# Edges of an attention stage: the last tile's softmax sums on the tensor engine, and the second image's normalisation moved forward

## The chip, the cores and the metric

The kernel runs on one core of a Trainium2 chip. A core has five engines with queues of their own: TensorE (PE, with weight loads shown as PEld), VectorE (DVE), ScalarE (ACT), GpSimd (POOL) and SyncE (SP), which here issues nearly all DMAs. The engines run side by side and wait for each other through semaphores. The metric is the device time of one execution in microseconds (us), lower being better; a profile is one execution recorded instruction by instruction.

## The reference

Two layers work on x of shape (2, 256, 64, 64), that is two images of 256 channels and 4096 tokens. Layer 0 is a Mamba block with an MLP behind a group norm. Layer 1 is attention with 8 heads of 32 channels behind another group norm. Only layer 1 is touched here:

```python
def _L1_conv_ref(x, qkv_w, qkv_b, num_heads):
    ...
    qkv = jnp.einsum('bchw,oc->bohw', x, qkv_w) + qkv_b[None, :, None, None]
    qkv = qkv.reshape(b, 3, num_heads, head_dim, n)
    q, k, v = (qkv[:, 0], qkv[:, 1], qkv[:, 2])
    scale = 1.0 / math.sqrt(head_dim)
    attn_logits = jnp.einsum('bhci,bhcj->bhij', q, k) * scale
    attn_weights = jax.nn.softmax(attn_logits, axis=-1)
    out = jnp.einsum('bhij,bhcj->bhci', attn_weights, v)
    return out.reshape(b, c, h, w)
...
x = x + _L1_conv_ref(_gn(x), L1_conv_qkv_w, L1_conv_qkv_b, 8)
```

## The kernel before

`conv_preact_kernel` runs `mamba_stage` for both images (to about 1993 us of the profile), then `attention`, then `out_of_range`, a check that decides whether a slower general version must run (it isn't run on this data). Inside `attention` the order of instructions on every engine is the order in which the code writes them (`tc.manual_schedule`), so the code is read as a schedule.

Attention takes an image as KG x NT = 16 query tiles: two groups of four heads, each with eight tiles of 512 queries. A tile walks over NC = 32 chunks of 128 keys, and a chunk has two halves of two heads each. For each half `logits` (L1162) makes scores on TensorE into one of three PSUM buffers `s`; `exponentials` (L1175) makes their exponentials on ScalarE; `values` (L1199) multiplies by v into `po`, 32 output rows for each head. The sums of the exponentials over the keys, the softmax's denominators, are gathered by `add_up`. Heads 0 and 1 are written into a buffer `chunk` that holds four terms side by side. After every third key chunk VectorE sums the four terms in one instruction (`sum_chunk`, L1184) into the first place of the next `chunk` buffer. There are two such buffers, so ScalarE can write into a buffer again only once the sum that read it is done. Heads 2 and 3 are added one by one: on GpSimd into `acc_p` (L1230, L1232), and for some chunks (SHARED) head 2 on VectorE into `acc_2` in PSUM (L1229).

When a tile is done, `finish` works through it in steps that are laid between the next tile's chunks by `side`: `Slots.run` is called once for each key chunk, and a step's `yield n` asks for the next one n turns later. The steps copy `po` out of PSUM (L1240), put the partial sums together (L1242, L1243), sum over the 128 key rows with a matrix of ones on TensorE (L1250), copy that out (L1253), take reciprocals in four pieces (L1257), multiply (L1260, on GpSimd except for the very last tile), add bias and the residual (L1263), store (L1264), and keep the largest sum and reciprocal for the range check (L1266, L1267).

For image 0, q, k and v were prepared by the Mamba stage. For image 1 they are made in `prepare`, between the two images: `load_x` (L1032) brings x, `normalise` (L1036) applies the group norm, `project` (L1046) makes q or k, `project_values` (L1067) makes v. The first two x tiles share one `q` buffer. The norm's two scales come from `group_norm_scales`: VectorE aggregates statistics (L39), TensorE averages over the channels of a group (L43), VectorE forms the spread (L45 to L51), TensorE averages again (L55), ScalarE takes a logarithm and an exponential (L58, L59). This generator is also run by `side`, from the first chunks of image 0. The loads and the first normalisation for image 1 are put into image 0's last tile by lines in `run`:

```python
                        if b == 0 and s == S - 8:
                            load_x(0)
                            load_x(1)
                        if b == 0 and s == S - 4:
                            normalise(0)
```

Here s counts key chunks over all tiles and S is their number, so S - 8 is chunk 24 of the last tile.

Of the kernel before, what the change touches and what calls it, by code (L numbers as in the profile page):

```python
# [11 lines left out]
F32 = mybir.dt.float32  # L12
F32R = mybir.dt.float32r
AF = mybir.ActivationFunctionType
ALU = mybir.AluOpType
AX = mybir.AxisListType
# [3 lines left out]
P = 128  # L20
T = 512
GROUP = 8
HEADS = 8
D = 32
QUAD = 4
KG = HEADS * D // P
# [3 lines left out]
def group_norm_scales(nc, small, psum_tile, stats, gmat, eps_t, out):  # L30

    KC = stats.shape[1]
    mv = [small.tile([P, 2], F32, name=f"gn_mv{k}") for k in range(KC)]
    e = [small.tile([P, 2], F32, name=f"gn_e{k}") for k in range(KC)]
    out += [small.tile([P, 2], F32, name=f"gn_sc{k}") for k in range(KC)]
    for k in range(KC):
        nc.vector.bn_aggr(mv[k], stats[:, k, :, :].rearrange("p a s -> p (a s)"))  # L39
    yield 2  # L40
    ps = psum_tile()
    for k in range(KC):
        nc.tensor.matmul(ps[:, k : k + 1], lhsT=gmat, rhs=mv[k][:, 0:1], start=True, stop=True)  # L43
    for k in range(KC):
        nc.vector.tensor_copy(out[k][:, 0:1], ps[:, k : k + 1])  # L45


    for k in range(KC):
        nc.vector.tensor_sub(e[k][:, 0:1], mv[k][:, 0:1], out[k][:, 0:1])
        nc.vector.tensor_mul(e[k][:, 1:2], e[k][:, 0:1], e[k][:, 0:1])  # L50
        nc.vector.tensor_add(e[k][:, 1:2], e[k][:, 1:2], mv[k][:, 1:2])  # L51
    yield 2
    ps = psum_tile()
    for k in range(KC):
        nc.tensor.matmul(ps[:, k : k + 1], lhsT=gmat, rhs=e[k][:, 1:2], start=True, stop=True)  # L55
    yield
    for k in range(KC):
        nc.scalar.activation(e[k][:, 0:1], ps[:, k : k + 1], AF.Ln, bias=eps_t)  # L58
        nc.scalar.activation(out[k][:, 1:2], e[k][:, 0:1], AF.Exp, scale=-0.5)  # L59
# [909 lines left out]
def attention(ctx, tc, stats, consts, w, outs, scratch, range_t):  # L969
# [8 lines left out]
    nc = tc.nc  # L978
    ident, gmat, _, eps_t = consts
    C, L = outs[0].shape  # L980
    KC = C // P
    NT = L // T
    NC = L // P
# [3 lines left out]
    wp = ctx.enter_context(tc.tile_pool(name="l1w", bufs=1))  # L987
    ps_s = ctx.enter_context(tc.tile_pool(name="l1pss", bufs=3, space=PSUM))
    ps_2 = ctx.enter_context(tc.tile_pool(name="l1ps2", bufs=1, space=PSUM))
# [4 lines left out]
    b_qkv = wp.tile([P, 3 * KC], F32, name="b_qkv")  # L994
    nc.sync.dma_start(b_qkv, w["qkv_b"].rearrange("(k p) -> p k", p=P))
    ones = wp.tile([P, D], F32, name="ones")
# [5 lines left out]
    p1 = ctx.enter_context(tc.tile_pool(name="l1p1", bufs=1))  # L1002
    p3 = ctx.enter_context(tc.tile_pool(name="l1p3", bufs=2))
    kq = ctx.enter_context(tc.tile_pool(name="l1kq", bufs=1))
    w_qkv = wp.tile([P, KC, 3 * C], F32, name="w_qkv")
    gn = []
    side = Slots()

    def s_tile():
        return ps_s.tile([P, 2, T], F32, name="s", tag="s")  # L1010
# [88 lines left out]
    def image(b):  # L1099

        x, out = scratch.image(b), outs[b]
# [84 lines left out]
        def values(first, end):  # L1186

            u = first
            while u < end:
# [8 lines left out]
                for h in range(4):  # L1198
# [5 lines left out]
                        stop=(c == NC - 1),  # L1204
                    )

        def add_up(s):
            i, c = divmod(s, NC)
            tile_ = tiles[i]
            eb = todo[s].e[1]  # L1210
            if c == NC - 2:
                tile_.acc = p1.tile([P, 3, T], F32, name="acc_sb")
                sum_chunk(s, tile_.acc[:, 0:2].rearrange("p h t -> p (h t)"))
            elif place(c) == 3:
                todo["chunk"] = chunk()
                sum_chunk(s, todo["chunk"].rearrange("p q h t k -> p q (h t) k")[:, 0, :, 0])
            if c == 0:
                tile_.acc_p = p3.tile([P, 2, T], F32, name="acc_p")
                tile_.eb0 = eb
                return  # L1220
            acc_p = tile_.acc_p
            if c == 1:
                nc.gpsimd.tensor_add(acc_p, tile_.eb0, eb)
            elif c in SHARED:
                if c == SHARED[0]:
                    tile_.acc_2 = ps_2.tile([P, T], F32, name="acc_2", tag="a2")
                    nc.vector.tensor_copy(tile_.acc_2, eb[:, 0, :])
                else:
                    nc.vector.tensor_add(tile_.acc_2, tile_.acc_2, eb[:, 0, :])  # L1229
                nc.gpsimd.tensor_add(acc_p[:, 1, :], acc_p[:, 1, :], eb[:, 1, :])  # L1230
            else:
                nc.gpsimd.tensor_add(acc_p, acc_p, eb)  # L1232

        def finish(i):

            g, t = divmod(i, NT)
            d = tiles[i]
            cols = bass.ts(t, T)
            po = p1.tile([P, T], F32, name="po_sb")
            nc.vector.tensor_copy(po, d.po)  # L1240
            acc = d.acc
            nc.vector.tensor_add(acc[:, 2, :], d.acc_2, d.acc_p[:, 0, :])  # L1242
            nc.vector.tensor_add(acc[:, 0:2, :], acc[:, 0:2, :], todo[i * NC + NC - 1].e[0])  # L1243
            res = p3.tile([P, T], F32, name="res")
            nc.sync.dma_start(res, x[g * P : (g + 1) * P, cols])
            yield 3
            ps = ps_2.tile([P, T], F32, name="sums_ps", tag="a2")
            for h in range(4):
                part = acc[:, h, :] if h < 3 else d.acc_p[:, 1, :]
                nc.tensor.matmul(ps[h * D : (h + 1) * D, :], lhsT=ones, rhs=part, start=True, stop=True)  # L1250
            yield
            sums = p1.tile([P, T], F32, name="sums")
            nc.vector.tensor_copy(sums, ps)  # L1253
            yield
            r = p1.tile([P, T], F32, name="r")
            for j in range(T // P):
                nc.vector.reciprocal(r[:, bass.ts(j, P)], sums[:, bass.ts(j, P)])  # L1257
                yield 2

            (nc.vector if b == 1 and i == KG * NT - 1 else nc.gpsimd).tensor_mul(po, po, r)  # L1260
            yield 2
            bias = b_qkv[:, 2 * KC + g : 2 * KC + g + 1]
            nc.vector.scalar_tensor_tensor(res, po, bias, res, ALU.add, ALU.add)  # L1263
            nc.sync.dma_start(out[g * P : (g + 1) * P, cols], res)  # L1264
            at = b * KG * NT + i
            nc.vector.tensor_reduce(range_t[:, 0, at : at + 1], sums, AX.X, ALU.max)  # L1266
            nc.vector.tensor_reduce(range_t[:, 1, at : at + 1], r, AX.X, ALU.max)  # L1267

        def run():
            k = 0  # L1270
            while k <= len(PHASES) or b == 1 and side.waiting:
                for p in PHASES[k] if k < len(PHASES) else ():
                    s, half = divmod(p, 2)
                    i, c = divmod(s, NC)
                    if half == 0:
                        if c == 0:
                            tiles[i] = Slot()
                            load_queries(i + 1)
                        if i % NT == NT - 1 and i < KG * NT - 1 and c % (T // P) == 0:

                            load_keys(i // NT + 1, c * P // T)
                        if b == 1 and 1 <= i <= KG:
                            nc.sync.dma_start(scratch.v[b * KG + i - 1, :, c, :], v[:, c, (i - 1) * P : i * P])
                        if b == 0 and s == S - 8:
                            load_x(0)
                            load_x(1)
                        if b == 0 and s == S - 4:
                            normalise(0)
                    if k > 0 or b == 0:
                        exponentials(s, half)  # L1290
                    if half == 1:
                        add_up(s)
                if b == 0 and k == len(PHASES):
                    project(0, 1)
                turns = 1
                if 0 < k <= len(PHASES):
                    units = PHASES[k - 1]
                    values(units[0], units[-1] + 1)
                    turns = sum(u % 2 for u in units)
                    if (units[-1] + 1) % (2 * NC) == 0:  # L1300
                        side.start(side.now, finish(units[-1] // (2 * NC)))
                for _ in range(turns):
                    side.run()
                phase_logits(k + 1)
                k += 1
# [18 lines left out]
    with tc.manual_schedule():  # L1324

        nc.scalar.preload_act_table_set(Plan.TABLES["exp"])
        images = [image(b) for b in range(2)]
        images[0].load()
        nc.sync.dma_start(w_qkv, w["qkv_wT"].rearrange("(k p) f -> p k f", p=P))

        side.start(1, group_norm_scales(nc, wp, lambda: ps_2.tile([P, T], F32, name="gn_ps", tag="a2"), stats[1], gmat, eps_t, gn))
        images[0].phase_logits(0)
        images[0].run()
        prepare(images[1])
        images[1].run()
# [176 lines left out]
```

## Time and profile before

| what | us |
|---|---|
| median of three runs | 4296.89 |
| the three runs | 4292.04, 4300.41, 4296.89 |
| the profiled execution | 4292.38 |
| its span, first to last instruction | 4290.6 |
| mean granted TensorE clock (share of full) | 0.985 |
| group norm's ScalarE work and waits, L58 and L59 | 2012.1 to 2020.2 |
| first image's last value matmuls and the projections begin | 3090.18 |
| last score matmul ends | 4266.35 |
| last exponential ends | 4267.92 |
| softmax sums of the last tile ready in PSUM | 4276.48 |
| last output store issued, landed | 4282.15, 4284.19 |
| range flag written by VectorE | 4284.71 |
| flag loaded by the other engines | 4284.8 |

The stretch from 1993 to 3090 is image 0's attention, from there to about 3190 image 1's projections, and then image 1's attention. Within an image the engines form one pipeline: TensorE, ScalarE, VectorE and GpSimd are each over 85% busy. After the last exponential only the last tile's ending is left, and its steps hang on each other. From the flag on, 5.8 us pass in which every engine loads the flag, branches and stops.

### The profile page before, as it was taken

To read this page: it belongs to the slowest core of one execution; us is meant where nothing else is said; L and a number is where in the kernel's file an instruction comes from. 1 tells how busy PE (TensorE), PEld (TensorE's weight loads), DVE (VectorE), ACT (ScalarE), POOL (GpSimd) and SP (SyncE) were. 2 spreads that over 40 slices of the span, in tenths; PEclk is the share of its full clock that TensorE was granted. 3 is DMA by queue.
4 is the path that set the end of the run, shared out by engine and by line. 5 is a ranking of instruction groups with operands and counts; after the bars stand their busy time and mean duration, and the time that the engine had idled before them with its cause. 6 is when DMAs were issued, how large, how long until landed. Compare 5 with 4: busy or idle time off the path is not lost.

```text
span 4290.6 us, 58937 instructions
## 1 busy us (share of the span) xinstructions
PE 4115.5 (96%) x21154; PEld 1799.6 (42%) x21154; DVE 3866.3 (90%) x3309; ACT 3727.0 (87%) x4982; POOL 3750.8 (87%) x1913
## 2 busy tenths in 40 slices
PE   6799999999999999988999999999999999999998
PEld 2233333333334333333444444444454444444443
DVE  5899999999999999995898989899858989898998
ACT  5789898998788888875999999999859999999997
POOL 3999999999899999994898888889728988888887
PEclk8899999999999999999999999999999999999999
DMA  6334333334444444447101040110182110401100
GB/s 212 107 114 130 117 115 123 128 128 133 150 146 160 162 141 140 143 166 167 33 18 28 18 106 18 28 30 21 50 253 54 32 28 18 106 22 25 29 21 9
DMA packets 172302, 389.58 MB, mean 91 GB/s; under 512 B 23392, under 2 KB 49760, under 8 KB 163808
## 3 DMA queue, kind: packets, MB, share of 16 engines
q1 hardware_dynamic: 171120, 383.37, 29.4%
q8 instruction: 168, 2.75, 0.3%
q10 hardware_dynamic: 880, 2.36, 0.3%
q14 instruction: 134, 1.10, 0.1%
HBM read 292.33 MB, written 93.32 MB: 90 GB/s over the span
## 4 chain that ended last, share of the span: by engine, by line
PE 79%; DVE 12%; ACT 4%; issue 3%; DMA 1%; POOL 1%; SPq 0%; DVEq 0%; POOLq 0%; ACTq 0%
PE s L1162 25%; PE po L1199 23%; PE mm L448 15%; DVE h L869 7%; PE mm L688 4%; PE y L901 4%; PE bn L448 2%; PE mm L647 2%; DVE bn L860 2%; ACT da L853 1%; PE s L1046 1%; PE y L899 1%; ACT L248 1%; PE sums_ps L1250 1%; PE mm L684 1%
## 5 line engine op out<-in xcount | busy, mean ns | idle before, releaser
L1184 DVE TENSOR_REDUCE chunk<-chunk 128x1024 f32<-128x4096 f32 x288 | 1269.8, 4409 | 176.4 <-ACT chunk L1175 174.7
L1232 POOL TENSOR_TENSOR acc_p<-acc_p,e 128x1024 f32<-128x1024 f32 x480 | 1167.3, 2432 | 124.1 <-ACT e L1175 99.4
L875 POOL TENSOR_TENSOR h<-h,c 128x1024 f32<-128x1024 f32 x512 | 1203.4, 2376 | 32.8 <-issue 15.7
L1175 ACT ACTIVATE e<-s 128x1024 f32<-128x1024 f32 x1056 | 1084.6, 1030 | 91.8 <-PE s L1162 56.7
L1162 PE MATMUL s<-q,k 128*128 128x512 f32 x4096 | 1155.8, 415 | 7.0 <-ACT chunk L1175 2.6
L1175 ACT ACTIVATE chunk<-s 128x1024 f32<-128x1024 f32 x992 | 1119.8, 1129 | 48.2 <-PE s L1162 22.9
L1199 PE MATMUL po<-chunk,v 128*32 128x512 f32 (+1 forms) x5248 | 1057.0, 521 | 0.0
L1199 PE MATMUL po<-e,v 128*32 128x512 f32 (+1 forms) x5504 | 1019.3, 500 | 1.5 <-ACT e L1175 1.5
L1162 PEld LDWEIGHTS s<-q,k 128*128 128x128 f32 x4096 | 714.3, 189 | 624.8 <-ACT e L1175 235.4
L853 ACT ACTIVATE da<-dt_rep,neg_a 128x512 f32<-128x512 f32 x1024 | 695.6, 702 | 105.8 <-DVE h L869 101.4
L1230 POOL TENSOR_TENSOR acc_p<-acc_p,e 128x512 f32<-128x512 f32 x480 | 621.8, 1295 | 94.7 <-ACT e L1175 64.8
L869 DVE TENSOR_TENSOR_SCAN h<-da,state,dbu 128x512 f32<-128x512 f32 x512 | 651.5, 1275 | 14.3 <-PE y L901 7.1
L869 DVE TENSOR_TENSOR_SCAN h<-da,state,bn 128x512 f32<-128x512 f32 x512 | 647.0, 1264 | 11.4 <-PE y L901 5.5
L864 POOL TENSOR_TENSOR dbu<-dtu_rep,b 128x1024 f32<-128x1024 f32 x176 | 417.8, 2374 | 17.0 <-issue 7.3
L448 PE MATMUL bn<-proj,pick 112*128 112x512 f32 x512 | 341.9, 669 | 87.9 <-DVE h L869 84.8
L248 ACT ACT_TABLE_LOAD x312 | 400.3, 1283 | 6.2 <-PEq L1502 0.7
L1199 PEld LDWEIGHTS po<-e,v 128*32 128x32 f32 x5504 | 251.8, 109 | 269.7 <-issue 104.4
L860 DVE TENSOR_TENSOR bn<-dtu_rep,bn 128x512 f32<-128x512 f32 x512 | 346.8, 680 | 16.8 <-PE bn L448 8.5
L1199 PEld LDWEIGHTS po<-chunk,v 128*32 128x32 f32 x5248 | 241.5, 108 | 250.7 <-issue 250.7
L1229 DVE TENSOR_TENSOR acc<-acc,e 128x512 f32<-128x512 f32 x448 | 309.6, 691 | 17.4 <-ACT chunk L1175 0.5
L901 PE MATMUL y<-h,sum 128*32 128x512 f32 x2048 | 302.0, 615 | 8.5 <-POOL h L875 8.3
L448 PE MATMUL mm<-yn,w_in 128*128 128x512 f32 x512 | 257.0, 627 | 8.2 <-ACT yn L538 3.6
(149 smaller groups left out, 4177.2 us busy)
## 6 DMA issues: line engine op xcount, KB each, us to landing
dt_rep<-dt_dram SPq DMA_DIRECT2D x128, 512.0 KB, 5.0
dtu_rep<-dtu_dram SPq DMA_DIRECT2D x128, 512.0 KB, 5.3
k<-qk_dram SPq DMA_DIRECT2D x62, 512.0 KB, 7.4
q<-qk_dram SPq DMA_DIRECT2D x124, 256.0 KB, 4.8
b<-bc_dram SPq DMA_DIRECT2D x64, 256.0 KB, 3.2
c<-bc_dram SPq DMA_DIRECT2D x64, 256.0 KB, 3.9
dt_dram<-dt SPq DMA_DIRECT2D x64, 256.0 KB, 2.2
dtu_dram<-lw SPq DMA_DIRECT2D x64, 256.0 KB, 3.7
```

What stands on the lines that cost most here:

```text
L248: self.nc.scalar.preload_act_table_set(self.TABLES[task.table])
L448: nc.tensor.matmul(out, lhsT=lhsT, rhs=rhs, start=(i == 0), stop=(i == len(pairs) - 1))
L853: nc.scalar.activation(da[j].tile, dt.tile[:, j, :], AF.Exp, scale=scale)
L869: nc.vector.tensor_tensor_scan(h.tile[:, j, :], da[j].tile, dbu, initial, ALU.mult, ALU.add)
L875: nc.gpsimd.tensor_tensor(h.tile, h.tile, rows_c.tile.unsqueeze(1).to_broadcast([P, 2, T]), ALU.mult)
L901: nc.tensor.matmul(y.tile[j * PQ : (j + 1) * PQ, :], lhsT=sum4, rhs=pair[j // 2].h.tile[:, j % 2, :], start=False, stop=(qd == NQ - 1),)
L1162: nc.tensor.matmul(ps[:, j, :], lhsT=keys[i // NT, kt][:, h, kj : kj + P], rhs=queries[i][:, h, :], start=True, stop=True)
L1175: nc.scalar.activation(e, todo[s].s[half], AF.Exp, scale=SCALE)
L1184: nc.vector.tensor_reduce(out, terms, AX.XY, ALU.add)
L1199: nc.tensor.matmul(tiles[i].po[h * D : (h + 1) * D, cols], lhsT=v[:, c, g * P + h * D : g * P + (h + 1) * D], rhs=todo[s].e[h // 2][:, h % ...
L1230: nc.gpsimd.tensor_add(acc_p[:, 1, :], acc_p[:, 1, :], eb[:, 1, :])
L1232: nc.gpsimd.tensor_add(acc_p, acc_p, eb)
```

## The change

Three things are changed. In `group_norm_scales` the first two `yield`s are altered and the generator is started one turn earlier, so that the averaging matmuls L43 and the steps L45 to L51 come earlier while the second matmuls and ScalarE's work keep their turns. The x loads for image 1 are written 16 key chunks earlier and the first normalisation 10 chunks earlier. The last tile of image 1 gets an ending of its own, `end`: its last chunk of four terms is no longer summed on VectorE, nor are the last partial sums put together. TensorE takes all terms as they are, in up to five matmuls for each head that add up in one PSUM tile, in part before the last value matmuls. The reciprocals and the multiplication read PSUM directly, the bias is added to the residual beforehand on ScalarE, and the final addition is on GpSimd.

```diff
@@ group_norm_scales
         nc.vector.bn_aggr(mv[k], stats[:, k, :, :].rearrange("p a s -> p (a s)"))
-    yield 2
+    yield
     ps = psum_tile()
...
         nc.vector.tensor_add(e[k][:, 1:2], e[k][:, 1:2], mv[k][:, 1:2])
-    yield 2
+    yield 4
     ps = psum_tile()
@@ image
+        def last(i):
+            return b == 1 and i == KG * NT - 1
+
         def add_up(s):
...
-            if c == NC - 2:
+            if last(i) and c == NC - 1:
+                return
+            if last(i) and c == NC - 2:
+                pass
+            elif c == NC - 2:
                 tile_.acc = p1.tile([P, 3, T], F32, name="acc_sb")
...
-            (nc.vector if b == 1 and i == KG * NT - 1 else nc.gpsimd).tensor_mul(po, po, r)
+            nc.gpsimd.tensor_mul(po, po, r)
...
+        def end():
+
+            i = KG * NT - 1
+            g, t = divmod(i, NT)
+            d = tiles[i]
+            res = p3.tile([P, T], F32, name="res")
+            nc.sync.dma_start(res, x[g * P : (g + 1) * P, bass.ts(t, T)])
+            ps = s_tile()[:, 0, :]
+            acc = p1.tile([P, T], F32, name="acc_end")
+            nc.vector.tensor_copy(acc, d.acc_2)
+            nc.scalar.activation(res, res, AF.Identity, bias=b_qkv[:, 2 * KC + g : 2 * KC + g + 1])
+            terms = [[todo[S - 2].chunk[:, k // 2, h, :, k % 2] for k in range(4)] for h in range(2)]
+            terms += [[d.acc_p[:, 0, :], acc], [d.acc_p[:, 1, :]]]
+
+            def sum_up(rounds):
+                for n in rounds:
+                    for h in range(4):
+                        n_ = n - 4 + len(terms[h])
+                        if 0 <= n_:
+                            part = terms[h][n_] if n_ < len(terms[h]) else todo[S - 1].e[h // 2][:, h % 2, :]
+                            nc.tensor.matmul(
+                                ps[h * D : (h + 1) * D, :], lhsT=ones, rhs=part, start=(n_ == 0), stop=(n == 4)
+                            )
+
+            sum_up(range(4))
+            yield
+            sum_up([4])
+            r = p1.tile([P, T], F32, name="r")
+            for j in range(T // P):
+                nc.vector.reciprocal(r[:, bass.ts(j, P)], ps[:, bass.ts(j, P)])
+            po = p1.tile([P, T], F32, name="po_sb")
+            nc.vector.tensor_mul(po, d.po, r)
+            nc.gpsimd.tensor_add(res, po, res)
+            nc.sync.dma_start(out[g * P : (g + 1) * P, bass.ts(t, T)], res)
+            at = b * KG * NT + i
+            nc.vector.tensor_reduce(range_t[:, 0, at : at + 1], ps, AX.X, ALU.max)
+            nc.vector.tensor_reduce(range_t[:, 1, at : at + 1], r, AX.X, ALU.max)
@@ run
-                        if b == 0 and s == S - 8:
+                        if b == 0 and s == S - 24:
                             load_x(0)
                             load_x(1)
-                        if b == 0 and s == S - 4:
+                        if b == 0 and s == S - 14:
                             normalise(0)
...
+                    ending = end() if b == 1 and k == len(PHASES) else iter(())
+                    next(ending, None)
                     values(units[0], units[-1] + 1)
+                    next(ending, None)
                     turns = sum(u % 2 for u in units)
-                    if (units[-1] + 1) % (2 * NC) == 0:
+                    if (units[-1] + 1) % (2 * NC) == 0 and not last(units[-1] // (2 * NC)):
                         side.start(side.now, finish(units[-1] // (2 * NC)))
@@ attention
-        side.start(1, group_norm_scales(nc, wp, lambda: ps_2.tile([P, T], F32, name="gn_ps", tag="a2"), stats[1], gmat, eps_t, gn))
+        side.start(0, group_norm_scales(nc, wp, lambda: ps_2.tile([P, T], F32, name="gn_ps", tag="a2"), stats[1], gmat, eps_t, gn))
```

## Prediction

> **What bounds the kernel now.** I read the page first, then the table of stretches over the attention part, then the timeline at the three places that the change touches, and last the chain of waits at the end.
>
> ```profile
> PE   4115.5 (96%) x21154; PEld 1799.6 (42%) x21154; DVE 3866.3 (90%) x3309; ACT 3727.0 (87%) x4982; POOL 3750.8 (87%) x1913
> ```
>
> TensorE (PE) is busy for 96% of the span, but that is an average. By stretch:
>
> ```profile
> 2012.00:2021.20 9.20, 5.37 (x24) 2.98 (x25) 6.95 (x5) 7.16 (x11) 2.40 (x2) 0.81 1.11 221
> ...
> 2100.00:3060.00 960.00, 958.71 (x6669) 450.05 (x6671) 869.60 (x510) 897.77 (x905) 845.51 (x454) 1.00 0.13 32
> ```
>
> The columns are stretch, length, then busy time of PE, PEld, DVE, ACT and POOL. Inside an image PE has 958.71 of 960 us: a delay or a gain of PE anywhere is kept to the end, because PE has no idle time in which to absorb it. The first stretch is the second image's group norm, and there PE has only 5.37 of 9.20 us.
>
> ```profile
> 2009.82 2.25 DVE L51 TENSOR_TENSOR gn_e<-gn_e,gn_mv 128x1 f32<-128x1 f32 x1
> ...
> 2012.12 1.28 ACT L58 ACT_TABLE_LOAD   x1
> ...
> 2014.74 0.56 PE L55 MATMUL gn_ps<-gn_e,gmat 128*128 128x1 f32 x2 [2.23 <-DVE gn_e L51]
> ...
> 2015.34 0.26 ACT L58 ACTIVATE gn_e<-gn_ps,eps_t 128x1 f32<-128x1 f32 x1 [1.94 <-PE gn_ps L55]
> ```
>
> An addition of one column takes 2.25 us. TensorE's second averaging matmul is late by it, and ScalarE then waits 1.94 us with the exponentials queued behind.
>
> The other place is the end of the first image. In an earlier query tile the trace shows what a late VectorE does:
>
> ```profile
> 2381.61 2.83 DVE L1263 SCALAR_TENSOR_TENSOR res<-po_sb,b_qkv,res 128x512 f32<-128x512 f32 x1
> ...
> 2386.15 4.40 DVE L1184 TENSOR_REDUCE chunk<-chunk 128x1024 f32<-128x4096 f32 x1
> ...
> 2390.64 1.08 ACT L1175 ACTIVATE chunk<-s 128x1024 f32<-128x1024 f32 x1 [1.33 <-DVE chunk L1184]
> ...
> 2391.78 0.73 PE L1162 MATMUL s<-q,k 128*128 128x512 f32 x2 [0.92 <-ACT chunk L1175]
> ```
>
> The sum over a chunk started 5.08 us after ScalarE had begun that chunk's last exponential (2381.07 in the timeline), ended at 2390.55, and only then was the buffer free: ScalarE lost 1.33 us, PE 0.92. In the last tile of the first image:
>
> ```profile
> 3063.83 4.41 DVE L1184 TENSOR_REDUCE chunk<-chunk 128x1024 f32<-128x4096 f32 x1
> ...
> 3085.38 2.31 DVE L1036 TENSOR_SCALAR q<-q,gn_sc 128x512 f32<-128x512 f32 x2
> ```
>
> The same sum starts at 3063.83, 2.64 us after its exponential at 3061.19, and the normalisation L1036 comes 21 us later. Project (L1046) starts at 3090.18, just as PE's last value matmuls end: it waits neither for x nor for L1036. At the end:
>
> ```profile
> 4274.47 2.00 PE sums_ps L1250 x8
> ...
> 4277.23 3.40 DVE r L1257 x4
> ...
> 4281.37 0.75 DVE res L1263
> ```
>
> The chain is VectorE work: the chunk sum (4267.08 to 4271.41), four single steps, the sums on PE (ended 4276.48), a copy, four reciprocals, two more steps, then the range check; the flag is written at 4284.71 and all engines load it at 4284.8.
>
> [...] the 2.25 us of L51 end with a GpSimd addition (2012.06), L1263 took 0.74 or 2.83 us by where it met one, and L1184 stays at 4.41. [...] Here the eight records of L1250, each 1.06 long, fill 2.00 us. [...]
>
> **The change part by part.**
>
> *A, group norm.* The two copies and six one-column steps of L45 to L51 now stand ahead of the first chunk sum on VectorE instead of behind it, and the first averaging matmuls (L43, 0.61 us) are one PE phase earlier. Nothing is added. The first pair then ends near 2002.2; [...] the six steps (0.16 each) end between 2004.9 and 2007.1. The second pair (L55) stands where it was and finds its data: ScalarE's 1.94 us go. The table load was already under way at 2012.12 and ends at 2013.40; that is the next thing late. What is queued behind the new order is the first chunk sum: it starts at about 4.9 rather than 3.58 (2007.1 at worst) and ends at 2009.3 (2011.5). ScalarE needs that buffer at 2010.99, so 0 to 0.5 us could come back. I take -1.9; ends -1.3 and -2.2 (the PE-side wait of 2.23).
>
> *B, x load and normalisation.* The two x loads go from chunk step 24 to 8 of the last tile and are moved past one output store (L1264) on SyncE's queue, which waits at most the 0.4 us that each issue takes (L1032 median 0.44); the query buffer has been free for a tile. No one waited for these loads, so they gain nothing. L1036 moves from before step 28 to before the chunk sum of step 18. Where it leaves, it hid behind PE's work (PE never waited there), so nothing is gained; and the end of that tile is no earlier. Where it arrives, [...] at 3085.38 such a pair took 0.73 and 1.66, each waiting out one addition. Here the first would end near 3064.7, a GpSimd addition of 1.29 goes in, and the second ends near 3066.25. The sum then starts 5.0 us after its exponential, as in the 2381 case (5.08): ScalarE is held 1.2, PE 0.8. Queued behind on VectorE are two additions and the next sum, late by as much but short of the next buffer need by about 0.2 us. I take +0.8. Ends: 0 (both in one gap) and +3 (the second behind an addition of 2.41, and the next sum late too).
>
> *C, the end.* Gone: chunk sum 4.41, L1240, L1242 and L1243 (0.68, 0.68, 1.22), copy L1253 (0.69), L1263 on VectorE (0.75). Added on PE: 15 matmuls of 32 rows (5, 5, 3 and 2 per head) instead of 4. A round of four such value matmuls goes at about 0.88 us per 512 columns (timeline from 3058.91 to 3060.5: one and a half rounds with their tail in 1.6). PE is free of the step-30 values at 4267.2; four rounds of sums take it to 4270.7, the last values to 4271.6, the last round to 4272.5. The two inputs made on other engines are there: GpSimd's at 4266.71, the copy acc_end after two additions of 0.69 at about 4268.5, used from 4269.8. So sums at 4272.6 rather than 4276.48: -3.9. Then reciprocals straight from PSUM 3.40 (no row shows them from PSUM; the copy L1253 from PSUM costs 0.69 as L1242 from SBUF costs 0.68, so equal; bound 3.2 to 3.8), multiplication 0.70: 4276.7. GpSimd's addition 1.29 (L1260's form, 1297 ns median) plus 0.06 handover: store issued at 4278.15 instead of 4282.15. It lands 2.04 us later by this store's own record (4284.19 before), at 4280.2. VectorE's flag goes on without the copy and L1263: about 4279.3. The built code lets every engine load the flag only after all DMAs have landed, so the landing, not the flag, is last: 4280.2 instead of 4284.8, and VectorE's own load, 0.25 later than the others before, is level. C: -4.7; ends -3.5 and -5.5. The new activation on res (0.7, ScalarE free from 4267.92) and its early load lie beside PE's sums.
>
> **Sum.** -1.9 + 0.8 - 4.7 = -5.8 us. The profiled execution took 4292.38 (span 4290.6 and 1.8 around it) and would take 4286.6. The median of the three runs is 4296.89, and they lie from 4292.04 to 4300.41; on it I predict 4291.1.
>
> **Rivals.** R1, *the new wait is larger*: GpSimd's additions meet the moved VectorE steps at both places; A gives -1.3, B costs +2.5: -3.5, 4293.4. For it: GpSimd was 87% busy and a waiting step costs up to 2.4. Against: both alignments are deterministic here and I followed them. R2, *the moved steps find gaps*: B 0, A -2.2, C -5.5 with the flag level with the landing: -7.7, 4289.2, and with the runs' scatter it can pass 0.2%. For it: GpSimd's pauses of 0.6 us near 2004. R3, *the sums do not share the array*: if the 15 sum matmuls run one after another, they cost 15 x 0.86 = 12.9 us instead of five rounds of 0.86 = 4.3, 8.6 more: C +3.9, all +2.8, 4299.7, slower than before. The place is TensorE between the last exponential and the reciprocals; it decides once that stretch is over 5.8 us longer than I count, that is above 10.1. Against it: L1250 and L1199 do run side by side in the trace. R4, *B does what its words say and saves time*: it would need a wait for x or for L1036 at 3090, and the trace has none. With L1036's 2.31 off the path and no stall it would give -8.9: 4288.0.
>
> **How the numbers follow.** The forecast (-4.5 to -7) has 0.55, R1 0.17, R2 0.21, R3 0.05, R4 0.02. About 0.2%, 8.6 us, is what a measurement of this kernel can tell from no change. The forecast, R1 and most of R2 lie inside; R2's far end, R4 and scatter on the forecast's side give 0.24 faster; R3 and scatter on R1 0.06 slower; 0.70 same. The range holds the bounds -2.5 to -8 and some 4 us of run-to-run scatter: 4285 to 4297.
>
> **What would show it.** A: L58 starts at about 2013.4 with no wait for L55. B: a wait of ScalarE for a chunk sum of about 1.2 us near 3070 and a PE gap below 1. C: PE's sums end about 6.2 us after the last score matmul (4266.35 to 4272.5 in old time), no chunk sum after the last exponential, the flag loads within 0.1 us of the landing. Wrong would be: PE idle inside the sums, reciprocals above 3.8 us, or a stall at 3070 above 2.

## The result, and the profile after

| | before | after |
|---|---|---|
| median, us (22 runs each) | 4295.51 | 4289.21 |
| lowest to highest | 4288.85 to 4300.41 | 4284.77 to 4297.99 |
| ratio, 95% interval | | 0.9987 [0.9981, 0.9993] |
| profiled execution, its span | 4292.38, 4290.6 | 4289.86, 4288.1 |

The changed kernel is faster by about 6 us, with an interval from 3.0 to 8.2 (the ratio's ends times 4295.51). The predicted gain was 5.8. The two profiled executions differ by only 2.5, and the first thing to find out is where the rest went. The totals of the page don't help. This is the line of the page after with each engine's busy us, share of the span and instructions.

```profile
PE 4119.0 (96%) x21176; PEld 1802.7 (42%) x21176; DVE 3855.6 (90%) x3304; ACT 3729.2 (87%) x4983; POOL 3751.9 (87%) x1913
```

Every share is what it was before. The gains and losses sit in four short places, so I laid the two traces over each other from the start of attention (before 1993.92, after 1996.24). The Mamba stage ahead of it ran 2.32 us longer in the execution after, with the same code in both kernels; that is scatter, and it hides nearly half of the gain in the profiled pair. A tile is taken to end with its last exponential. From the start of attention on, "after minus before" runs like this:

| from attention's start to | after minus before, us | what lies in between |
|---|---|---|
| first exponential after the group norm | -2.05 | the norm's steps are earlier |
| end of query tile 0 | +0.04 | the 2.05 are lost again |
| end of tile 4 | -0.17 | slow drift |
| end of tile 5 | -1.37 | a wait of 1.3 us in tile 5, in before only |
| end of tile 14 | -1.76 | slow drift |
| projections begin | -0.76 | a larger wait behind the moved normalisation, +1.0 |
| end of image 1's first tile | -0.55 | image 1's start |
| end of tile 30 | -1.17 | slow drift |
| last score matmul | -0.06 | a wait of 1.3 us in tile 31, in after only |
| flag loaded | -5.17 | the new ending, -5.1 |

Of the steps in the middle nothing is left at the last score matmul. All of the profile's gain is the ending.

*The group norm.* The timeline after shows start, length, engine, line, operation and, in brackets, the idle time before it and what ended it.

```profile
2004.58 0.23 DVE L45 COPY gn_sc<-gn_ps 128x1 f32<-128x1 f32 x2 [8.04 <-PE gn_ps L43]
2004.77 1.57 DVE L49 TENSOR_TENSOR gn_e<-gn_mv,gn_sc 128x1 f32<-128x1 f32 x1
...
2007.10 4.41 DVE L1184 TENSOR_REDUCE chunk<-chunk 128x1024 f32<-128x4096 f32 x1
...
2013.68 0.60 PE L55 MATMUL gn_ps<-gn_e,gmat 128*128 128x1 f32 x4
...
2014.35 1.28 ACT L58 ACT_TABLE_LOAD   x1
2015.64 0.26 ACT L58 ACTIVATE gn_e<-gn_ps,eps_t 128x1 f32<-128x1 f32 x1
...
2020.40 1.01 ACT L1175 ACTIVATE e<-s 128x1024 f32<-128x1024 f32 x1
...
2021.45 1.07 PE L1199 MATMUL po<-e,v 128*32 128x256 f32 x4 [4.16 <-ACT e L1175]
```

The six small steps now come ahead of the chunk sum at 2007.10, L55 waits for nothing, and L58 starts as soon as its table is loaded: as predicted. But the last line differs from before, where it was

```profile
2021.17 0.63 PE L1199 MATMUL po<-e,v 128*32 128x256 f32 x4 [1.48 <-ACT e L1175]
```

The same matmuls took 0.63 there after a wait of 1.48. Here they take 1.07 after a wait of 4.16. The table of stretches shows why; its columns are the stretch, its length, busy time of PE, PEld, DVE, ACT and POOL, TensorE's granted clock, DMA share and GB/s. First after:

```profile
2021.40:2024.00 2.60, 2.55 (x8) 1.45 (x9) 0.68 (x1) 2.17 (x4) 2.38 (x2) 0.50 1.08 214
2024.00:2027.00 3.00, 3.00 (x16) 1.16 (x18) 2.16 (x2) 2.74 (x3) 2.42 (x2) 0.50 0.98 201
2027.00:2030.00 3.00, 3.00 (x22) 1.35 (x18) 2.78 (x2) 1.57 (x2) 1.64 (x2) 0.99 1.17 271
```

and before:

```profile
2015.10:2018.10 3.00, 3.00 (x11) 1.96 (x15) 3.00 (x1) 2.71 (x4) 0.00 (x0) 0.50 0.94 194
2018.10:2021.10 3.00, 1.59 (x12) 0.32 (x12) 0.92 (x1) 2.96 (x6) 0.00 (x0) 0.98 1.23 237
2021.10:2023.00 1.90, 1.74 (x8) 0.76 (x8) 0.00 (x0) 1.90 (x4) 1.74 (x1) 1.00 0.95 203
```

In both kernels TensorE runs at half clock for a while. Before, that was from 2015.1 to 2018.1, while ScalarE was still busy with its tables, and PE idled afterwards anyway (1.59 of 3.00): the slow stretch was free. After, PE's two waits (2.23 and 1.48) have become one of 4.16, and the half clock comes just when PE is the engine that everybody waits for.

*The x load and normalisation*, tile 15 of image 0, after:

```profile
3064.39 2.29 DVE L1036 TENSOR_SCALAR q<-q,gn_sc 128x512 f32<-128x512 f32 x2
...
3066.61 4.41 DVE L1184 TENSOR_REDUCE chunk<-chunk 128x1024 f32<-128x4096 f32 x1
...
3071.11 1.08 ACT L1175 ACTIVATE chunk<-s 128x1024 f32<-128x1024 f32 x1 [1.10 <-PE s L1162]
...
3072.24 0.73 PE L1162 MATMUL s<-q,k 128*128 128x512 f32 x2 [0.70 <-ACT chunk L1175]
```

The chunk sum starts 4.85 us after its exponential began (3061.76 in the timeline), ends at 3071.02, and ScalarE's next exponential into that buffer follows at once. Its wait is put down to a score matmul, but the sum's end is what fits.

*The wait that changed its tile.* A residual addition that meets a GpSimd addition makes a chunk sum late, in tile 5 before and in tile 31 after:

```profile
4239.98 2.77 DVE L1270 SCALAR_TENSOR_TENSOR res<-po_sb,b_qkv,res 128x512 f32<-128x512 f32 x1
...
4248.96 1.08 ACT L1175 ACTIVATE chunk<-s 128x1024 f32<-128x1024 f32 x1 [1.29 <-DVE chunk L1184]
```

It is the form quoted in the prediction from 2381, at another place, for the same price: L1270 takes 2.77 us here, while a GpSimd addition runs from 4239.80 to 4242.21, against a median of 0.74. The edits don't touch this code, and the two cancel (-1.20, +1.11). Which part of the change moves it, the experiments tell.

*The end.* The chain of waits after, then the timeline from the reciprocals on:

```profile
4268.62 1.05 PE po L1199 x5
4269.67 3.22 PE s L1296 x14
...
4274.22 0.92 PE s L1296 x2
4275.14 0.03 issue
4275.16 3.40 DVE r L1305 x4
```

```profile
4278.59 0.69 DVE L1307 TENSOR_TENSOR po_sb<-po,r 128x512 f32<-128x512 f32 x1
...
4279.41 1.26 POOL L1308 TENSOR_TENSOR res<-po_sb,res 128x512 f32<-128x512 f32 x1 [10.41 <-DVE po_sb L1307]
...
4280.70 0.34 SPq L1309 DMA_DIRECT2D out<-res  x1
...
4281.73 0.14 DVE L1404 CAST range_flag_i<-range_flag 1x1 int32<-1x1 f32 x1
```

Before, the chain from the last score matmul to the reciprocals was VectorE's, with the chunk sum of 4.4 us and four more steps in it. Now it is TensorE's alone. Counted from the end of the last score matmul, the sums end after 6.45 us (4268.62 to 4275.07) instead of 10.13, the reciprocals start after 6.54 instead of 10.88, and the flag is written after 13.25 instead of 18.36.

The clock has a share in this too. The stretch of the sums before, then the last of them after:

```profile
4274.45:4276.50 2.05, 1.93 (x8) 0.20 (x8) 0.00 (x1) 0.00 (x0) 0.00 (x0) 0.50 0.00 0
```

```profile
4274.20:4275.15 0.95, 0.88 (x7) 0.00 (x0) 0.00 (x0) 0.00 (x0) 0.00 (x0) 1.00 0.00 0
```

Before, PE had waited 5.45 us for VectorE when it began the four sums, and that round ran at half clock in 2.00 us. After, PE goes from the scores straight through to the sums: five rounds of sums and the last round of values take 5.56 us (4269.51 to 4275.07) at full clock, 0.93 a round.

### The profile page after: what moved, and what is told of

It reads as the page before. It is cut to its first block, busy times and chain, and to the rows that moved or that the text cites. A ratio compares the mean times of both kernels' runs of the same rounds, so it can differ in the third digit from the quotient of the medians.

```text
span 4288.1 us, 58982 instructions
## 1 busy us (share of the span) xinstructions
PE 4119.0 (96%) x21176; PEld 1802.7 (42%) x21176; DVE 3855.6 (90%) x3304; ACT 3729.2 (87%) x4983; POOL 3751.9 (87%) x1913
## 4 chain that ended last, share of the span: by engine, by line
PE 82%; DVE 10%; ACT 3%; issue 2%; DMA 1%; POOL 1%; SPq 0%; DVEq 0%; POOLq 0%; ACTq 0%
PE s L1162 25%; PE po L1199 24%; PE mm L448 16%; DVE h L869 6%; PE y L901 4%; PE mm L688 4%; PE bn L448 2%; PE mm L647 2%; DVE bn L860 1%; PE s L1046 1%; PE y L899 1%; PE mm L684 1%; PE sums_ps L1257 1%; ACT da L853 1%; ACT L248 1%
```

## The experiments

The theory from these traces was: the ending is worth 5 us by itself; the earlier group norm gives its 2 us back because TensorE is at half clock after its long wait; the moved load costs 1. The rival was that the ending gives less and the earlier group norm does pay in most executions, the traced one being a bad draw. Times below count from the start of attention and are minus those of before's profile. A ratio is against runs of the kernel before on the same chip.

**The ending alone**: the changed kernel with A and B undone.

```diff
-    yield
+    yield 2
...
-    yield 4
+    yield 2
...
-                        if b == 0 and s == S - 24:
+                        if b == 0 and s == S - 8:
...
-                        if b == 0 and s == S - 14:
+                        if b == 0 and s == S - 4:
...
-        side.start(0, group_norm_scales(...))
+        side.start(1, group_norm_scales(...))
```

> Part C alone: the new ending, with the group norm, the x loads and the normalisation where they were before. If the ending carries the whole change: flag loaded about 15.6 us after the last exponential begins instead of 17.9, or, from the last score matmul, 5.1 us earlier than before; run time about 5 us below the kernel before (ratio near 0.9988). If group norm's 1.9 us are kept as predicted, this one is 1.1 us slower than the full change (-1.9 + 0.8 missing), that is -4.7 only.

Measured: 4288.48, ratio 0.9986 [0.9979, 0.9992]. The trace stays within 0.32 of before at every tile, is at +0.12 at the last score matmul, then at -4.16 at the reciprocals and -4.95 at the flag. The whole change has 0.9987: as far as the runs can tell, the ending is all of it.

**The group norm alone**: before with only A's three `yield` and start edits.

> Part A alone: group norm's steps earlier. Theory 1 (clock): the exponential after the norm starts 1.9 to 2.1 us earlier measured from the start of attention, TensorE then has waited over 4 us, runs at about half its clock for some 5 us, and by key chunk 11 of the first tile the gain is down to 0.2 or less; time unchanged. Theory 2 (as predicted): the 1.9 us are still there at the end of the first tile and at the last score matmul, but for single later stalls.

Measured: 4293.72, ratio 1.0002 [0.9994, 1.0011]. That interval ends 2.6 us below before, so the time alone can't exclude a gain of 1.9. The trace can. In its timeline the matmuls behind the tables, and in the table of stretches the clock:

```profile
2019.94 1.07 PE L1199 MATMUL po<-e,v 128*32 128x256 f32 x4 [4.83 <-ACT e L1175]
```

```profile
2019.94:2022.94 3.00, 3.00 (x9) 1.80 (x10) 0.69 (x1) 2.57 (x3) 2.83 (x2) 0.50 1.05 209
```

The gain is 1.81 at the first exponential and 0.33 at the end of the tile. A's loss doesn't come from B or C. This trace also moves the wait from tile 5 to tile 31. So do all eight traces that have A, as far as tile 5 goes: none of them has the wait there, and the three without A (before, the ending alone, the load alone) have it. In tile 31 it stands in the six traces with A that leave the range reductions where they were, and in no other. It is A, then, that moves this wait; how it does so is not shown.

**The load alone**: before with only B's two conditions.

> Part B alone: x loads and first normalisation earlier. As predicted: nothing gained, ScalarE held once near key chunk 22 of the first image's last tile by 1 to 1.3 us and TensorE by 0.7 to 0.9; the projections begin 0.8 to 1.0 us later than before measured from the start of attention. Rival (the stall in the profile after was chance): no such wait and the projections within 0.2 us of before.

Measured: 4295.52, ratio 1.0000 [0.9992, 1.0008]. The same wait in tile 15 as in the full change, where before has none:

```profile
3072.64 1.08 ACT L1175 ACTIVATE chunk<-s 128x1024 f32<-128x1024 f32 x1 [1.10 <-PE s L1162]
```

It costs 1.0 up to the projections (+1.10 to +2.09). Two more losses came along: a wait in tile 2 (+1.0) behind a late residual addition, and +1.1 at image 1's start, where this trace has a clock of 0.50 (3183 to 3186) and before has 1.00 (3181 to 3184). The flag is 3.01 later in the trace, but the runs together show no difference, so of the three only the one in tile 15 is put down to B: it is in all six traces that have B and in none of the five without it.

**Filling TensorE's wait.** If the wait lowers the clock, work for TensorE in the wait must keep it up, even work whose result nobody reads. Behind L55, 12 matmuls with the matrix `gmat` go into a spare score buffer, and in a second kernel 24 (none of the kernel's own work is left out).

```diff
+    fill = spare()
+    for _ in range(12):        # 24 in the second
+        nc.tensor.matmul(fill[:, 0, 0:P], lhsT=gmat, rhs=gmat, start=True, stop=True)
     yield
```

> The changed kernel with twelve more matmuls of the constant matrix by itself behind the second averaging matmuls; their result is not read. TensorE is busy about 3 us longer in the time in which it waits for ScalarE's table loads. Theory 1 (clock): the wait shrinks from 4.16 to about 1 us, the clock stays near full, and the 1.9 to 2.0 us gained at the norm are still there at key chunk 11 and at the end of the first tile. Theory 2 (something other than the clock takes the gain back, such as the score buffers or the DMA load at that time): the added work does nothing or costs time, and the gain is again near 0 by key chunk 11.

> As the kernel with twelve more matmuls of the constant matrix, with twenty-four, about 5.8 us of TensorE work whose result is not read. TensorE's wait at the norm was 2.85 us with twelve and the kernel kept 0.7 of 1.8 us. Theory 1 (clock): the wait is gone, no stretch there at half clock, and 1.5 to 1.9 us are kept at key chunk 11 and the end of the first tile, less what the added work pushes out itself. Theory 2: again below 0.7.

With 12 the wait shrinks to 2.85 and the clock still drops, to 0.59 in the 3 us behind the wait and 0.84 in the 3 us after those; in the change it is 0.50 up to 2027:

```profile
2021.09 0.62 PE L1202 MATMUL po<-e,v 128*32 128x256 f32 x4 [2.85 <-ACT e L1178]
```

With 24 there is no wait, and the clock is full from the first stretch on:

```profile
2012.69 5.61 PE L58 MATMUL s<-gmat 128*128 128x128 f32 x48
```

```profile
2018.00:2021.00 3.00, 3.00 (x25) 1.54 (x23) 0.00 (x0) 2.99 (x5) 0.89 (x1) 1.00 1.10 218
```

With 12, 0.69 of 1.80 us are kept to the end of the tile; with 24, 1.82 of 1.97. The times are 4289.43, ratio 0.9989 [0.9983, 0.9996], and 4287.49, ratio 0.9988 [0.9979, 0.9996]: not to be told from the change itself. Nor does the gain with 24 stay: at the flag its trace is only 0.2 us ahead of the change's. Of the lead of 1.8 at the end of tile 0 some 0.6 went at image 1's start and the rest bit by bit between the tiles. What the filling shows, it shows up to the end of the first tile.

**Shortening the wait.** The same theory says that ScalarE's four table loads of 1.28 us should be cut, for then the wait is short without any filling. They come from the order logarithm, exponential, logarithm, exponential. Both logarithms first leave two loads:

```diff
         nc.scalar.activation(e[k][:, 0:1], ps[:, k : k + 1], AF.Ln, bias=eps_t)
+    for k in range(KC):
         nc.scalar.activation(out[k][:, 1:2], e[k][:, 0:1], AF.Exp, scale=-0.5)
```

> The changed kernel with both logarithms of the group norm first and both exponentials after, so two table loads instead of four. ScalarE's work there falls by two loads of 1.28, to about 3.5 us, and TensorE's wait from 4.16 to about 1.6. Theory 1 (clock): with so short a wait the clock does not fall [...], so not only the 2.6 us of the loads but also the 1.9 us that the change had lost again are kept: 3.9 to 4.6 us ahead of before at key chunk 11 and at the end of the first tile. Theory 2 (the loss has another cause): only 2.6 us ahead there, since the change alone was at 0.

```profile
2010.51 1.28 ACT L58 ACT_TABLE_LOAD   x1
2011.80 0.41 ACT L58 ACTIVATE gn_e<-gn_ps,eps_t 128x1 f32<-128x1 f32 x2
...
2014.79 0.63 PE L1200 MATMUL po<-e,v 128*32 128x256 f32 x4 [1.34 <-ACT e L1176]
```

```profile
2014.79:2017.79 3.00, 2.86 (x18) 1.34 (x22) 0.83 (x2) 3.00 (x4) 2.83 (x2) 1.00 1.06 221
```

Measured: 4284.26, ratio 0.9979 [0.9973, 0.9986]. The wait is 1.34, the clock stays at 1.00, and of 4.79 us at the first exponential 4.77 are there at the end of the tile. The five traces in a row:

| kernel | PE's wait | mean clock of the 3 us after it | ahead at first exponential | kept at end of tile 0 |
|---|---|---|---|---|
| group norm alone | 4.83 | 0.50 | 1.81 | 0.33 |
| the change | 4.16 | 0.50 | 2.05 | -0.04 |
| with 12 matmuls in it | 2.85 | 0.59 | 1.80 | 0.69 |
| two table loads | 1.34 | 1.00 | 4.79 | 4.77 |
| with 24 matmuls in it | none | 1.00 | 1.97 | 1.82 |

The loss goes with the half clock, whether the wait was filled or shortened; with one trace for each kernel, A's mechanism is shown. The last two kernels below, which have two table loads as well, agree: 4.90 of 4.89 and 4.43 of 4.52 us kept at the end of tile 0, and in the first of them a wait of 1.34 with the four matmuls behind it taking 0.63. "A bad draw" falls for A: all four traces with A, four table loads and a wait left over (the three in the table and the one with the sums on VectorE, further down, 1.8 to 0.3) lost most of it.

**Sums of the last tile on VectorE, the rest of the ending kept**: what of C is TensorE's sums, and what the rest (no copy out of PSUM, the last addition on GpSimd)?

```diff
-            acc = p1.tile([P, T], F32, name="acc_end")
-            nc.vector.tensor_copy(acc, d.acc_2)
+            acc = d.acc
+            nc.vector.tensor_add(acc[:, 2, :], d.acc_2, d.acc_p[:, 0, :])
+            nc.vector.tensor_add(acc[:, 0:2, :], acc[:, 0:2, :], todo[S - 1].e[0])
...
-            sum_up(range(4))
             yield
-            sum_up([4])
+            for h in range(4):
+                part = acc[:, h, :] if h < 3 else d.acc_p[:, 1, :]
+                nc.tensor.matmul(ps[h * D : (h + 1) * D, :], lhsT=ones, rhs=part, start=True, stop=True)
```

> The changed kernel with the last tile's sums put together on VectorE as before (chunk sum, two additions, four matmuls), but with the rest of the new ending: no copies out of PSUM, bias added ahead on ScalarE, last addition on GpSimd. If the sums taken on TensorE carry the ending's gain, about 3.3 of its 5.1 us are gone and the flag is loaded about 2 us earlier than before measured from the last score matmul (a copy of po 0.6, the copy of the sums 0.7, the last addition 0.7). Rival: the shorter chain of single steps carries it, and 4 us or more stay.

Measured: 4290.71, ratio 0.9998 [0.9990, 1.0007]. The old chain is back in its timeline, chunk sum first and PE waiting for VectorE's last addition:

```profile
4270.47 4.41 DVE L1184 TENSOR_REDUCE acc_sb<-chunk 128x1024 f32<-128x4096 f32 x1
...
4277.56 1.07 PE L1288 MATMUL s<-acc_sb,ones 128*32 128x512 f32 x3 [5.15 <-DVE acc_sb L1282]
...
4279.58 3.39 DVE L1291 RECIPROCAL r<-s 128x128 f32<-128x128 f32 x4 [2.17 <-PE s L1288]
```

From the last score matmul on this ending gains 1.81 at the flag, the full one 5.1: the sums on TensorE carry 3.3. About 1.1 of it is the slower round: here PE has waited 5.15 us, and its one round of sums takes 2.03 us (4277.56 to 4279.58), like the 2.00 at a clock of 0.50 before, instead of 0.93.

**All that helped together**: the ending, the earlier norm with two table loads, B undone, and the range reductions of `finish` two turns later, so that a late residual addition has fewer steps between it and the chunk sum.

```diff
             nc.sync.dma_start(out[g * P : (g + 1) * P, cols], res)
+            yield 2
             at = b * KG * NT + i
```

> The new ending and group norm of the change with two table loads, the x loads and the normalisation back where they were before, and the two range reductions of each tile two turns after its last addition, so that they no longer stand in front of the same chunk sum. If the parts add up: 4 us from the norm, none of the about 1 us near key chunk 22 of the first image's last tile, no ScalarE wait of 1.3 us for a chunk sum anywhere, and 5 from the ending: 9 to 11 us below the kernel before (ratio 0.9975 to 0.9979), 4 to 5 below the changed kernel. If the waits for chunk sums were not caused by this cluster, one of 1.3 us is still there.

Measured: 4282.53, ratio 0.9978 [0.9969, 0.9987]. Tile 15 has no wait now, the 4.9 of the norm are kept, and a late residual addition of 2.74 us costs no more than 0.5 of waiting. But at image 1's start 1.2 us are lost: PE waits 2.18 there, 2.19 in before, and this time the clock drops (0.50 from 3174.90 to 3177.90).

```profile
3173.54 0.73 PE L1163 MATMUL s<-q,k 128*128 128x512 f32 x2 [2.18 <-DVE chunk L1058]
3174.11 5.30 PE L1068 MATMUL s<-w_qkv,e 128*128 128x256 f32 x16
```

**The same with that wait filled too**: 9 unread matmuls ahead of image 1's first scores.

```diff
+                fill = ps_2.tile([P, T], F32, name="fill", tag="a2")
+                for _ in range(9):
+                    nc.tensor.matmul(fill[:, 0:P], lhsT=gmat, rhs=gmat, start=True, stop=True)
                 image.ahead()
```

> The kernel with all parts together, and nine matmuls of the constant matrix (about 2.2 us, result not read) in front of the second image's first score matmuls, where TensorE waits 2.2 us for VectorE in every trace and in some of them (the load alone, the filled one, the sums on VectorE, all together) ran the next 3 us at half clock. Theory 1 (clock): no stretch at half clock at the second image's start, so the 1.2 to 1.7 us that all together lost between its projections and its second tile shrink to 0.7 or less; the time equal or up to 1.5 us lower. Theory 2 (the loss there is the wait itself or the loads at that time): lost as before, or more by the added matmuls.

```profile
3181.28 0.73 PE L1166 MATMUL s<-q,k 128*128 128x512 f32 x2 [0.18 <-DVE chunk L1058]
3182.34 3.72 PE L1068 MATMUL s<-w_qkv,e 128*128 128x256 f32 x16 [0.33 <-ACT chunk L1179]
```

The same 16 matmuls take 3.72 instead of 5.30, and the loss from the projections to the end of tile 16 is 0.3 instead of 1.2. That the filling did it is not shown by this one trace: in six of the ten traces without it they take 3.62. Measured: 4284.61, ratio 0.9977 [0.9968, 0.9987]. Against the kernel without filling the time shows nothing; these two and the kernel with two table loads alone are equal within their intervals. The cheapest of the three, one line on top of the change, is the one to keep: 0.9979 against the change's 0.9987. Their intervals overlap by 0.0005, so that it beats the change rests on the traces too, where its flag is 9.13 earlier than before's and the change's 5.17.

## Why the prediction was right, and where not

The forecast was the likeliest case and held: -5.8 predicted, -6.3 between the medians, within 0.2% and in the range. Its parts did not all hold.

*A, -1.9 predicted, 0 measured.* Each step up to the first exponential was right: the one-column steps end at 2007.18, which is 2004.85 in the time of before (2.33 less), the early end of the predicted 2004.9 to 2007.1; no wait at L55; 2.05 us gained there. The step that failed is the reading of the PE row, "a delay or a gain of PE anywhere is kept to the end, because PE has no idle time in which to absorb it". PE can also lose a gain, by running slower: the same four matmuls took 1.07 instead of 0.63. Behind the longest and the shortest waits of the table above the clock was 0.50 (4.16 and 4.83) and 1.00 (1.34). It also fell after waits of 2.23, in the kernel before, and of 2.85, with 12 matmuls; after 2.19 it fell in some traces and not in others (last section). The view that would have warned me was in reach: the granted clock of 0.81 in the first stretch that the prediction quotes, and beside it 0.50 from 2015.1 to 2018.1. I read the row for PE's busy time and passed over its clock. Had I asked where the half clock falls once the two waits of PE, 2.23 and 1.48, become one, A would have been near 0.

*B, +0.8 predicted, +1.0 measured.* The mechanism is the one predicted: the pair takes 2.29 us beside GpSimd's additions (1.00 at 3099.14 in before, where none runs), the sum starts about 5 us after its exponential, ScalarE waits 1.10 (1.2 predicted), PE 0.70 (0.8). That B has no gain is shown by the load alone and by the full set without it; x and the normalisation were never late.

*C, -4.7 predicted, -5.1 measured.* (The prediction's own times, 4280.2 instead of 4284.8, give -4.6.) The sums were counted to end 6.2 us after the last score matmul, and took 6.45; the reciprocals straight from PSUM were 3.40 as assumed; the store was issued 12.08 us after that matmul, predicted 11.8. One step failed: "the landing, not the flag, is last". The store lands about 2.0 us after 4280.70, and the engines load the flag at 4281.94, just after VectorE wrote it and before the landing. So the flag, 5.1 earlier, sets the end, not the landing, which is only 3.7 earlier relative to the last score matmul (17.84 to 14.11). The rival with serial sums (R3) is out: it needs 12.9 us for the 15 sums, and they and the last values together took 5.56. The prediction priced a round at 0.88, not at the 2.00 that it quotes for L1250, and was right to; that the 2.00 was half clock it did not say.

*Sum.* A's missing 1.9 was made good by nothing that the change does: C's extra 0.4 and B's 0.2 the other way leave -4.1 for the parts as measured, and the medians have -6.3 with an interval from 3.0 to 8.2. Both lie in it. That the total came so near with a third of it missing is luck as far as these runs tell, and a right total is weak evidence for its terms here; only the traces tell that one of the three was wrong.

Left open: why the drift between tiles goes in steps of 0.05 to 0.1 us in some traces (the change) and not in others (the ending alone), how A changes the tile in which a residual addition meets GpSimd, and why the end after the flag took 6.2 us instead of 5.9. There is one profile per kernel only.

## What to carry to other kernels

Before pricing a wait that goes away, look at the granted clock behind it: joining two short waits of TensorE, here 2.23 and 1.48 us, into one of 4.16, with the half clock behind it, cost as much as the work that was saved, and a slow stretch that was hidden before may come to stand in front of everybody. At the end of a program, where steps hang on each other, what counts is the chain's number of handovers and passes over the data: an engine with idle time took over sums that another could only do after the last input, and, busy throughout, ran a round of them in 0.93 us at a clock of 1.00, not in 2.00 at 0.50 as after the wait of 5.45. Edits that aim at different places are priced from traces, each alone; a total that comes out right says little of them.

## What the runs showed of the hardware

The same wait can cost or not. At image 1's start PE waits 2.18 or 2.19 us in every trace that has no filling there. The 16 matmuls after it then take 3.62 us in six of these ten traces (before, the change, the ending alone, the norm alone, two table loads, 24 matmuls), 4.75 in the load alone, 4.98 with 12 matmuls, and 5.30 in the sums on VectorE and in all together. PE's busy time around the wait doesn't tell them apart. In before:

```profile
3178.00:3181.00 3.00, 0.81 (x4) 0.57 (x4) 1.47 (x2) 2.09 (x3) 0.00 (x0) 1.00 0.81 313
3181.00:3184.00 3.00, 3.00 (x16) 2.64 (x15) 0.00 (x0) 1.57 (x2) 0.00 (x0) 1.00 1.04 311
```

and in the load alone:

```profile
3180.00:3183.00 3.00, 0.81 (x5) 0.33 (x3) 1.50 (x2) 2.02 (x3) 0.00 (x0) 0.98 0.75 292
3183.00:3186.00 3.00, 3.00 (x7) 2.44 (x8) 0.00 (x0) 2.30 (x3) 0.00 (x0) 0.50 1.00 343
```

PE is busy for 0.81 of the 3 us around the wait in both, and the 3 us behind it have the full clock in one and the half clock in the other. What decides between the two is not shown here. The clocks read above and here, by the length of the wait ahead of them: 1.00 after 1.34 (two table loads) and 1.48 (before); 1.00 in before and 0.50 in the load alone after 2.19; 0.50 after 2.23 (before), 0.59 after 2.85 (12 matmuls), 0.50 after 4.16 (the change), 4.83 (the norm alone) and 5.45 (the sums in before). With 9 unread matmuls in the wait at image 1's start the one trace taken has 3.72 for the 16 matmuls.

Logarithm and exponential in turn load a table each time, 1.28 us each and four loads in the change, though they follow each other in the same few instructions; ordering them by function saved two loads, and with them 2.6 us of ScalarE and the half clock, for one line.
